# A two-layer block on one core: the first sequence's norm, first chunk and first four scans moved into the end of layer 0

## The chip, the cores and the metric

The kernel runs on one core of one Trainium2 chip. A core has five engines with an instruction queue each: TensorE (PE: matrix products, with PEld for its weight loads), VectorE (DVE), ScalarE (ACT), GpSimd (POOL) and SyncE (SP, which here only issues transfers). Each queue is worked off in its order; between queues there are semaphores. The metric is the device time of one execution in microseconds; lower is better.

## The reference, cut to what matters

Four sequences of 256 tokens with 512 features pass through two layers. `ln` is a layer norm without weights.

```python
# layer 0
xn = ln(x)
x = x + attention(xn) + (silu(xn @ Wg.T) * (xn @ Wu.T)) @ Wd.T      # 32 heads, 1792 hidden
# layer 1
xn = ln(x)
px, z = split(xn @ in_proj, 2)                       # 1024 channels each
xc = silu(conv4(px))                                 # causal, 4 taps along time
dt_r, B, C = rmsnorm of the three parts of xc @ x_proj.T      # 32, 16, 16
dt = softplus(dt_r @ dt_proj.T + dt_bias)
h[t] = exp(dt[t] * -exp(A_log)) * h[t-1] + dt[t] * B[t] * xc[t]   # 16 states per channel
y = (sum over states of h * C + D * xc) * silu(z)
x = x + y @ out_proj.T + experts(xn)                 # a dense product and 8 LoRA experts, top 2
```

The recurrence over time runs along the free dimension of one instruction, the scan.

## The kernel before, in words

The order of the work is written out by hand. In layer 0 generators hand out the products of the feed-forward part in small portions (`go(ff, n)`) between the steps of attention; `gate_up(th)` makes the hidden values of half `th` (two sequences), split into a high and a low part (hhi, hlo) that are multiplied in two passes. Its weights come in blocks of 128 hidden rows (tile wgu), loaded by POOL's queue through a ring of five tiles, four blocks ahead (`load_w`, L367). After both halves of `gate_up`, `down(th, i)` forms one block of 128 tokens: one product with the attention output (L404), 14 pairs of products (hhi and hlo, L409), and an addition to x on VectorE (L413). A portion is one pair, or the first product, or the addition: 16 portions a block, 64 for the four blocks of `down(1)`.

Those 64 portions are spread through the beginning of layer 1, which begins with the first two token blocks (the first sequence), whose x is already final. In order: statistics, root, scaling (`norm_stats`, `norm_scale`), transposing by TensorE and copying to xn1T (`norm_turn`, `norm_copy`); for four pairs of channel chunks p the products px (`px_mm`, L648), the convolution on ScalarE, VectorE and POOL (`conv_in` L656 to L664, `conv_taps` L672 and L678); silu; the decay rates aneg (L970) from the tile al, which 16 small transfers fill (L561); the product pp (`pp_mm` L692) and its norm; `step_in`, `step_exp`, `step_out`, `step_x` for dt and dt times xc (du).

A scan works on a step u: one chunk of 128 channels (c) and a quarter g of its 16 states. The 128 partitions of a step are 32 channels of four states, and four such groups lie along the free dimension, 4 x 256 values. So dt and du must be spread: `send` writes them to DRAM, and `spread` reads every row four times (L773, L779). Then `decays` makes the decay factors (ScalarE, L802), `scan_in` multiplies bx into PSUM (VectorE, L808), `scan` runs the recurrence (VectorE, L820) and multiplies by C (POOL, hc, L824), `states_sum` sums states by TensorE (ysum, L834 and L836) and `close_chunk` multiplies by the gate (L840). There are 32 steps for each sequence, 128 in all. The scheduled remainder of layer 1 (gates, products with z, the next sequence's norm and products) hangs on step numbers by `put(b, s, f, ...)`: f is issued at step s of sequence b.

What sets the order around the change: layer 0's tiles (pool l0: hidden values, wd) take up the memory into which the pool act goes, with two of three decay tiles, h, hc and the late weights rl, bw, lb, ow. So all 64 portions are issued before `l0.close()`, except for the last, which is an addition, and scan 0 follows. PSUM is a second tie: three buffers (psmm) hold all products of 512 values, whatever stage they belong to.

Of the kernel before, what the change touches and what calls it, by code (L numbers as in the profile page):

```python
# [28 lines left out]
NG = 4  # L29
# [12 lines left out]
def block_kernel(  # L42
# [52 lines left out]
    pssc = ps0.enter_context(tc.tile_pool(name="pssc", bufs=2, space=PSUM))  # L95
    psav = ps0.enter_context(tc.tile_pool(name="psav", bufs=1, space=PSUM))

    att = ExitStack()
# [133 lines left out]


    qs, kms = {}, {}

# [128 lines left out]
    def load_w(i):  # L364
        if i < 2 * NW:
            t = ffn.tile([P, HC, P], F32R, tag="wgu", name="wgu", bufs=5)
            nc.gpsimd.dma_start(t, wgu_d[i % NW // 2, :, i % 2])  # L367
            wgus[i] = t

    def gate_up(th):  # L370
# [4 lines left out]
        for m in range(MC):  # L375
            for k in range(2):
                i = th * NW + 2 * m + k
                load_w(i + 4)
                if th == 0 and k == 0 and m % 2 == 1:
# [76 lines left out]
    fold.close()  # L456
    for i in range(4):
        load_w(i)
# [62 lines left out]
    attention(2, ff, True, 10, 4)  # L521
    attention(3, ff, False, 10, 4)
    go(ff)
# [13 lines left out]
    PER = DC * NU  # L537
    xns, xcs, nrms, dts, szs, crows = {}, {}, {}, {}, {}, {}

# [5 lines left out]
    w_of = {}  # L545
    w_of["x", 0, 0] = weights(inx_d, 0)
    vec = w1.tile([P, DC, V_END], F32, name="vec")
    nc.sync.dma_start(vec, vec_d)
    w_of["x", 0, 1] = weights(inx_d, 2)
    xpw = w1.tile([P, DC, 64], F32, name="xpw")  # L550
    nc.sync.dma_start(xpw, xp_d)
    lnw = w1.tile([64, 1], F32, name="lnw")
    nc.sync.dma_start(lnw, lnw_d)
    dtw = w1.tile([RK, DIN], F32, name="dtw")
    nc.sync.dma_start(dtw, dtw_d)
    w_of["x", 0, 2] = weights(inx_d, 4)

    al = w1.tile([P, DC, NG, NST], F32, tag="u", name="al")
    for n in range(NG):
        for k in range(NG):  # L560
            nc.sync.dma_start(  # L561
                al[n * NB : (n + 1) * NB, :, k, :],
                vec_d[k * NB : (k + 1) * NB, :, V_AL : V_AL + NST],
            )
    aneg = w1.tile([P, DC, NG, NU], F32, name="aneg")
# [65 lines left out]
    def norm_turn(b, i):  # L631
# [3 lines left out]
        live["pt", b, i] = pt  # L635

    def norm_copy(b, i):
        if i == 0:
            xns[b] = odd(b).tile([P, HC, S], F32, tag="xn1T", name="xn1T")
        nc.scalar.copy(xns[b][:, :, i * P : (i + 1) * P], live["pt", b, i])  # L640
# [155 lines left out]


    def decays(u):
        b, c, g = u // PER, u % PER // NU, u % NU
        da = decay[u % len(decay)]  # L800
        for k in range(NG):
            nc.scalar.activation(da[:, k, 1:], live["dts", b, c][:, k, 1:], AF.Exp,  # L802
                                 scale=aneg[:, c, k, g : g + 1])
# [9 lines left out]
    def scan(u, parts=1):  # L813
        b, c, g = u // PER, u % PER // NU, u % NU
        da, bx = decay[u % len(decay)], live["bx"]
        h = act.tile([P, NG, S], F32, tag="h", name="h", bufs=2)
        hc = act.tile([P, NG, S], F32, tag="hc", name="hc", bufs=3)
        for k in range(parts):
            n = slice(k * NG // parts, (k + 1) * NG // parts)
            nc.vector.tensor_tensor_scan(  # L820
                h[:, n].rearrange("p n t -> p (n t)"), da[:, n].rearrange("p n t -> p (n t)"),
                bx[:, n].rearrange("p n t -> p (n t)"), 0.0, ALU.mult, ALU.add,
            )
            nc.gpsimd.tensor_tensor(  # L824
                hc[:, n], h[:, n],
                crows[b][:, g, :].unsqueeze(1).to_broadcast([P, NG // parts, S]), ALU.mult,
            )
        live["hc", u] = hc
# [17 lines left out]
    def router(b, i):  # L846
# [3 lines left out]
        for hc in range(HC):  # L850
            mm(pr, lhsT=xns[b + i // 2][:, hc, i % 2 * P : (i % 2 + 1) * P], rhs=rl[:, hc, :],
               start=(hc == 0), stop=(hc == HC - 1))
# [62 lines left out]
    def dense(b, i, k):  # L915
        if k == 0:
            live["po", b, i] = psmm.tile([P, D], F32, tag="mm", name="po1")
        for hc in (2 * k, 2 * k + 1):
            mm(live["po", b, i], lhsT=xns[b][:, hc, i * P : (i + 1) * P], rhs=bw[:, hc, :],
               start=(hc == 0), stop=False)  # L920

    def expert_out(b, i):
        mm(live["po", b, i], lhsT=ident, rhs=x[:, 2 * b + i, :], start=False, stop=False)
        mm(live["po", b, i], lhsT=live["mt"][:, i * P : (i + 1) * P], rhs=lb,
           start=False, stop=False)

    def out_mm(b, i, c):
        mm(live["po", b, i], lhsT=xcs[b][:, c, i * P : (i + 1) * P], rhs=ow[:, c, :],  # L928
           start=False, stop=(c == DC - 1))
# [13 lines left out]
    exp_set()  # L943
    norm_stats(0)
    ff = (0 for i in range(4) for _ in down(1, i))
    go(ff, 6)
    norm_scale(0)
    for i in range(2):
        norm_turn(0, i)
        norm_copy(0, i)  # L950
    go(ff, 3)
    for p in range(NP):
        for i in range(2):
            px_mm(0, p, i)
        conv_in(0, p)
        conv_taps(0, p)
        if p == 0:
            load_x(0, 3)
            for c in range(DC):
                nc.gpsimd.tensor_scalar(  # L960
                    dgs[:, c, :], ident, vec[:, c, V_D : V_D + 1], 1.0, ALU.mult, ALU.mult
                )
        elif p < 3:
            load_z(0, p - 1)
            go(ff, 4 - p)
    conv_silu(0)
    go(ff, 14)
    for n in range(NG):
        w = slice(n * NB, (n + 1) * NB)
        nc.scalar.activation(  # L970
            aneg[w], al[w].rearrange("p c k (g n) -> p c k g n", n=NG)[:, :, :, :, n], AF.Exp
        )
    nc.gpsimd.tensor_scalar(aneg, aneg, -1.0, 1.0, ALU.mult, ALU.mult)
    pp_mm(0, 0)
    pp_mm(0, 1)
    pp_square(0)
    pp_norm(0)
    go(ff, 6)
    for q in range(2):
        step_in(0, 0, q)  # L980
        step_exp(0, 0, slice(2 * q, 2 * q + 2))
        for k in range(3):
            step_out(0, 0, q, k)
        step_x(0, q)
        spread("dt", 0, q)
        spread("du", 0, q)
    b_rows(0, 0)
    c_rows(0, 0)
    go(ff, 4 * (MC + 2) - 35)
    scan_in(0)  # L990
    l0.close()
    act = ctx.enter_context(tc.tile_pool(name="act", bufs=1))
    decay_tile(act)
    decay_tile(act)
    bw = act.tile([P, HC, D], F32, name="bw")
    rl = act.tile([P, HC, NE + P], F32, name="rl")
    lb = act.tile([P, D], F32, name="lb")
    ow = act.tile([P, DC, D], F32, name="ow")
    nc.sync.dma_start(rl, rl_d)
    nc.sync.dma_start(bw, base_d)  # L1000
    nc.sync.dma_start(lb, lb_d)
    nc.sync.dma_start(ow, ow_d)

# [10 lines left out]
    for b in range(B):  # L1014
# [14 lines left out]
        else:  # L1029
            for p in range(2):  # L1030
                for i in range(2):
                    put(b, 2 * p + i, pz_mm, b, p, i)
        put(b, 0 if b else 3, gate_silu, b, 0, 1)

        put(b, 1, step_in, b, 1, 0)
        put(b, 2, step_in, b, 1, 1)
        put(b, 3 if b else 4, step_exp, b, 1)
        for q in range(2):
            for k in range(3):
                put(b, 5 + 3 * q + k, step_out, b, 1, q, k)  # L1040
        for p in (2, 3):
            put(b, 3 * p + 2, step_x, b, p)
        for c in range(2, DC):
            put(b, 4 * c - 6, spread, "dt", b, c)
            put(b, 4 * c - 4, spread, "du", b, c)
        put(b, 10, load_z, b, 2)
# [6 lines left out]
        if nxt < B:  # L1053
            put(b, 0, norm_stats, nxt)
            put(b, 2, norm_scale, nxt)
            put(b, 3, norm_turn, nxt, 0)
            put(b, 4, norm_copy, nxt, 0)
            put(b, 4, norm_turn, nxt, 1)
            put(b, 5, norm_copy, nxt, 1)
            for p in range(NP):  # L1060
                put(b, 2 * p, load_x, nxt, p)
                for i in range(2):
                    put(b, 6 + 2 * p + i, px_mm, nxt, p, i)
                put(b, 8 + 2 * p, conv_in, nxt, p)
                put(b, 9 + 2 * p, conv_taps, nxt, p)
            put(b, 16, conv_silu, nxt, (b, 2))
            put(b, 17, pp_mm, nxt, 0)
            put(b, 18, pp_mm, nxt, 1)
# [40 lines left out]
    late = []  # L1109
    decays(0)  # L1110
    decays(1)
    b_rows(0, 1)
    c_rows(0, 1)
    for u in range(total + 2):
        if u + 2 < total:
            decays(u + 2)
# [11 lines left out]
        if u < total:  # L1128
            scan(u, 1 if u < total - 1 else 4)
            if u == 0:  # L1130
                go(ff)
        for f, a in late_at.get(u, ()):
# [112 lines left out]
```

## Time and profile before

| | us |
|---|---|
| median of 3 runs | 901.28 (899.8 to 903.99) |
| the profiled execution, its own time | 900.89 |
| its span, first to last instruction | 899.1 |
| busy: PE, DVE, ACT, POOL | 751.5, 677.3, 523.3, 493.6 |
| last product of layer 0 ends | 379.42 |
| first scan starts | 380.02 |
| scan h (L820), x131 | 292.5, mean 2.235 |
| bx (L808), x128 | 157.6, mean 1.231 |
| hc (L824), x131 | 301.9, mean 2.307 |

Times in the profile count from the first instruction. A group's line gives source line, engine, operation, output and inputs by the program's names, the number of instructions, busy time, mean duration, and the idle time ahead of them with what ended it. A line of the timeline gives start and duration; neighbouring instructions of one kind are merged. One execution is profiled, so a difference is taken from its rows and carried over to the median of the runs.

### The profile page before, as it was taken

The numbers are of one execution on the slowest core, as the hardware profiler recorded it, in microseconds if no ns is written. First come the engines' busy times: TensorE is split into PE (matmuls) and PEld (weight loads), VectorE is DVE, ScalarE is ACT, GpSimd is POOL, SyncE is SP. The second block draws the span as 40 slices with busy tenths as digits, with TensorE's granted clock in tenths as the row PEclk, the third lists the DMA queues.
The fourth block names the chain that finished last, engine by engine and source line by source line (L and its number), as shares of the span: only waits on it lengthen the run. The fifth ranks groups of instructions, "written<-read, shape, count | busy, mean of one in ns | idle before, by whom it ended". The sixth has DMA issues, their size and how long they took to land.

```text
span 899.1 us, 10412 instructions
## 1 busy us (share of the span) xinstructions
PE 751.5 (84%) x3538; PEld 432.3 (48%) x3538; DVE 677.3 (75%) x660; ACT 523.3 (58%) x1004; POOL 493.6 (55%) x375
## 2 busy tenths in 40 slices
PE   5999979999989989967795798687898768975875
PEld 3665545666556666734452444343444434422321
DVE  5685553476662422298998999999999989999996
ACT  4234455313436445597677596777686785764661
POOL 4222222001223323459966879868789749697665
PEclk9899999999999999988886999887999888889997
DMA  7232232001123142593522543532546322437310
GB/s 222 60 93 71 82 107 71 12 1 36 47 59 82 47 106 69 143 280 95 162 80 62 156 132 111 139 95 88 159 128 161 83 82 74 117 95 167 86 28 24
DMA packets 68608, 87.98 MB, mean 98 GB/s; under 512 B 12190, under 2 KB 53418, under 8 KB 68171
## 3 DMA queue, kind: packets, MB, share of 16 engines
q1 hardware_dynamic: 59194, 68.44, 27.0%
q0 software_dynamic: 9072, 18.35, 7.3%
q8 instruction: 28, 0.46, 0.2%
q10 hardware_dynamic: 288, 0.52, 0.2%
q14 instruction: 26, 0.20, 0.1%
HBM read 67.63 MB, written 10.49 MB: 87 GB/s over the span
## 4 chain that ended last, share of the span: by engine, by line
PE 46%; DVE 30%; ACT 14%; issue 5%; POOL 4%; DMA 1%; SPq 0%; DVEq 0%; ACTq 0%; POOLq 0%
DVE h L820 18%; ACT decay L802 6%; PE po L409 6%; DVE bx L808 6%; PE pu L384 5%; PE pg L384 4%; PE sc L296 4%; PE av L338 3%; POOL hc L824 3%; PE scT L328 3%; PE pz L788 2%; PE pp L692 2%; PE px L648 2%; PE ysum L836 2%; PE po L928 2%
## 5 line engine op out<-in xcount | busy, mean ns | idle before, releaser
L824 POOL TENSOR_TENSOR hc<-h,cr 128x1024 f32<-128x1024 f32 (+1 forms) x131 | 301.9, 2307 | 110.2 <-DVE h L820 96.9
L820 DVE TENSOR_TENSOR_SCAN h<-decay,bx 128x1024 f32<-128x1024 f32 (+1 forms) x131 | 292.5, 2235 | 13.2 <-POOL hc L824 0.8
L802 ACT ACTIVATE decay<-dts,aneg 128x255 f32<-128x255 f32 x512 | 217.1, 498 | 123.9 <-DVE h L820 115.6
L808 DVE TENSOR_TENSOR bx<-brow,dus 128x1024 f32<-128x1024 f32 x128 | 157.6, 1231 | 9.0 <-DMA dus<-dud 5.2
L836 PE MATMUL ysum<-hc,stack 128*32 128x256 f32 x1024 | 89.9, 421 | 88.1 <-POOL hc L824 88.0
L396 POOL TENSOR_TENSOR hlo<-g,hhi 128x512 fp32r<-128x512 f32 x28 | 36.1, 1290 | 146.9 <-ACT hhi L395 146.9
L298 DVE TENSOR_REDUCE mpl<-sc 128x4 f32<-128x1024 f32 x64 | 77.2, 1222 | 23.9 <-PE sc L296 23.8
L836 PEld LDWEIGHTS ysum<-hc,stack 128*32 128x32 f32 x1024 | 21.5, 111 | 147.6 <-POOL hc L824 129.3
L367 POOL DMA_DIRECT2D wgu<-in_wgu x56 | 31.1, 557 | 92.4 <-PE pg L384 83.0
L330 ACT ACTIVATE pe<-scT 128x1024 f32<-128x1024 f32 x64 | 62.8, 1023 | 31.6 <-PE scT L328 31.4
L928 PE MATMUL po<-ow,xc 128*128 128x512 f32 x128 | 71.4, 667 | 2.7 <-DVE xc L840 2.7
L648 PE MATMUL px<-xn1T,w_in 128*128 128x256 f32 x256 | 67.5, 415 | 7.1 <-ACT xn1T L640 5.7
L788 PE MATMUL pz<-xn1T,w_in 128*128 128x256 f32 x256 | 66.7, 406 | 0.0
L648 PEld LDWEIGHTS px<-xn1T,w_in 128*128 128x128 f32 x256 | 52.4, 208 | 27.7 <-issue 10.4
L392 DVE SCALAR_TENSOR_TENSOR g<-g,pg 128x512 f32<-128x512 f32 x28 | 19.2, 684 | 55.0 <-ACT g L391 55.0
L788 PEld LDWEIGHTS pz<-xn1T,w_in 128*128 128x128 f32 x256 | 47.9, 197 | 18.8 <-issue 12.3
L395 ACT CAST hhi<-g 128x512 fp32r<-128x512 f32 x28 | 17.4, 620 | 61.0 <-DVE g L394 60.5
L384 PE MATMUL pg<-xhi,wgu 128*128 128x512 f32 x112 | 46.8, 418 | 5.5 <-issue 2.9
L409 PE MATMUL po<-wd,hhi 128*128 128x512 f32 x112 | 50.2, 448 | 0.0
L384 PE MATMUL pu<-xhi,wgu 128*128 128x512 f32 x112 | 47.6, 425 | 2.3 <-issue 1.5
L296 PE MATMUL sc<-km,qg 128*128 128x512 f32 x128 | 43.9, 424 | 3.3 <-ACT pe L330 2.8
L678 POOL TENSOR_TENSOR xc<-xc,tap 128x256 f32<-128x256 f32 x48 | 34.9, 727 | 21.0 <-ACT tap L664 18.5
(178 smaller groups left out, 1246.2 us busy)
## 6 DMA issues: line engine op xcount, KB each, us to landing
dts<-dtd SPq DMA_DIRECT2D x128, 128.0 KB, 2.8
dus<-dud SPq DMA_DIRECT2D x128, 128.0 KB, 3.0
wgu<-in_wgu POOLq DMA_DIRECT2D x56, 256.0 KB, 2.7
w_in<-in_inx SPq DMA_DIRECT2D x16, 512.0 KB, 4.7
w_in<-in_inz SPq DMA_DIRECT2D x16, 512.0 KB, 5.6
dtd<-dt SPq DMA_DIRECT2D x16, 256.0 KB, 2.3
dud<-du SPq DMA_DIRECT2D x16, 256.0 KB, 2.3
wd<-in_wd POOLq DMA_DIRECT2D x7, 512.0 KB, 3.6
```

Source lines behind the costliest of these rows:

```text
L296: mm(sc[:, hp, :], lhsT=qs[b][:, gq, hf, qb * P : (qb + 1) * P], rhs=kms[b][:, 2 * hp : 2 * hp + 2, :], start=True, stop=True)
L298: nc.vector.tensor_reduce(mpl2[b % 2][:, qb, :, 16 + 2 * gq + hf].rearrange("p (a i) -> p a i", a=2), sc.rearrange("p a (i k) -> p a i k", ...
L384: mm(ps, lhsT=wgus[i][:, hc, :], rhs=xs[j][:, hc, :], start=(hc == 0 and j == 0), stop=(hc == HC - 1 and j == 1))
L409: mm(po, lhsT=hids[th][j][:, m, i * P : (i + 1) * P], rhs=wd[:, m, :], start=False, stop=(m == MC - 1 and j == 1))
L648: mm(px[:, i, :], lhsT=w[:, i, hc, :], rhs=xns[b][:, hc, :], start=(hc == 0), stop=(hc == HC - 1))
L788: mm(pz[:, i, :], lhsT=w[:, i, hc, :], rhs=xns[b][:, hc, :], start=(hc == 0), stop=(hc == HC - 1))
L802: nc.scalar.activation(da[:, k, 1:], live["dts", b, c][:, k, 1:], AF.Exp, scale=aneg[:, c, k, g : g + 1])
L808: nc.vector.tensor_tensor(bx, brow[g // 2][:, g % 2, :].unsqueeze(1).to_broadcast([P, NG, S]), live["dus", b, c], ALU.mult)
L820: nc.vector.tensor_tensor_scan(h[:, n].rearrange("p n t -> p (n t)"), da[:, n].rearrange("p n t -> p (n t)"), bx[:, n].rearrange("p n t -> ...
L824: nc.gpsimd.tensor_tensor(hc[:, n], h[:, n], crows[b][:, g, :].unsqueeze(1).to_broadcast([P, NG // parts, S]), ALU.mult,)
L836: mm(ysum[k * NB : (k + 1) * NB, :], lhsT=stack, rhs=hc[:, k, :], start=False, stop=(g == NU - 1))
L928: mm(live["po", b, i], lhsT=xcs[b][:, c, i * P : (i + 1) * P], rhs=ow[:, c, :], start=False, stop=(c == DC - 1))
```

## The change

Three parts. The layer norm of the first sequence and its transposes move from the beginning of layer 1 into attention 3 of layer 0 (`pre_stats`, `pre_scale`, `pre_turn`, called between that attention's eight steps), with xn1T of the even sequences in a pool of its own; the weight ring of `gate_up` has four tiles and loads three blocks ahead. The first chunk's dt and du are no longer sent through DRAM: TensorE multiplies them with selection matrices (sel, in the tile of the conv taps), VectorE copies the results; the second chunk still goes through DRAM. The decay, h and hc of steps 0 to 3 lie in tiles borrowed from layer 1's weights and temporaries (`lend`), so that these scans need not wait for the pool act: 12 portions of `down` are issued with step 0, 12 with step 1, the remaining 8 with step 2, and `open_act` follows scan 2. To make room, much moves: the transfers into al, xpw, lnw and dtw are issued after px 0 and the fourth load of px weights; dgs ahead of the products; aneg ahead of the last pair's convolution, which is done without POOL; silu in two parts; the z weights and gates of the first sequence at steps 2 to 8; its second half of dt, and the next sequence's norm and products, one to three steps later.

```diff
+    def pre_stats(i):
+        ...
+        nc.vector.bn_stats(st, x[:, i, :])
+        nc.vector.bn_aggr(first_ln["mv"][:, i, :], st)
+    def pre_scale():
+        mv, rs = first_ln["mv"], first_ln["rs"]
+        nc.scalar.activation(rs[:, 0:2], mv[:, 0:2, 1], AF.Sqrt, bias=eps[:, 0:1])
+        nc.scalar.preload_act_table_set("exp_and_others")
+        nc.vector.reciprocal(rs[:, 0:2], rs[:, 0:2])
+        for i in range(2):
+            first_ln[i] = ap1.tile([P, D], F32, tag="ln_xn", name="xn", bufs=2)
+            nc.vector.tensor_scalar(
+                first_ln[i], x[:, i, :], mv[:, i, 0:1], rs[:, i : i + 1], ALU.subtract, ALU.mult
+            )
+    def pre_turn(i):
+        if i == 0:
+            xns[0] = pre.tile([P, HC, S], F32, tag="xn1T", name="xn1T")
+        pt = psmm.tile([P, HC, P], F32, tag="mm", name="pt")
+        for hc in range(HC):
+            nc.tensor.transpose(pt[:, hc, :], first_ln[i][:, hc * P : (hc + 1) * P], ident)
+        nc.vector.tensor_copy(xns[0][:, :, i * P : (i + 1) * P], pt)
...
-            t = ffn.tile([P, HC, P], F32R, tag="wgu", name="wgu", bufs=5)
+            t = ffn.tile([P, HC, P], F32R, tag="wgu", name="wgu", bufs=4)
...
-                load_w(i + 4)
+                load_w(i + 3)
...
-    attention(3, ff, False, 10, 4)
+    attention(3, ff, False, 10, 4, [(pre_stats, 0), (pre_stats, 1), (pre_scale,), (pre_turn, 0),
+                                    (pre_turn, 1)])
...
-    w_of["x", 0, 0] = weights(inx_d, 0)
+    for i in range(2):
+        nc.sync.dma_start(t[:, i], inx_d[:, i])
...
-    al = w1.tile([P, DC, NG, NST], F32, tag="u", name="al")
+    al = w1.tile([P, NG, DC, NST], F32, tag="u", name="al")
+    def load_rest():
+        for n in range(NG):
+            for k in range(NG):
+                nc.sync.dma_start(
+                    al[n * NB : (n + 1) * NB, k],
+                    vec_d[k * NB : (k + 1) * NB, :, V_AL : V_AL + NST],
+                )
+        nc.sync.dma_start(xpw, xp_d)
+        ...
...
+    lent = {
+        "d": ("d", "w_in", "d", "w_in"), "h": ("w_in", "u", "w_in", "u"),
+        "hc": ("w_in", "lw", "e", "lw"),
+    }
...
-    norm_stats(0)
     ff = (0 for i in range(4) for _ in down(1, i))
-    go(ff, 6)
-    norm_scale(0)
-    for i in range(2):
-        norm_turn(0, i)
-        norm_copy(0, i)
-    go(ff, 3)
+    go(ff, 9)
+    for c in range(DC):
+        nc.gpsimd.tensor_scalar(
+            dgs[:, c, :], ident, vec[:, c, V_D : V_D + 1], 1.0, ALU.mult, ALU.mult
+        )
     for p in range(NP):
         for i in range(2):
             px_mm(0, p, i)
         if p == 0:
             load_x(0, 3)
+            load_rest()
+        if p < 3:
+            conv_in(0, p)
+            conv_taps(0, p)
+            go(ff, 1)
...
...
+    px = live["px", 0, 3]
+    nc.scalar.copy(pads[1][:, :, KC - 1 :], px)
+    for i in range(2):
+        v = vec[:, 6 + i, :]
+        nc.scalar.activation(px[:, i, :], px[:, i, :], AF.Identity, bias=v[:, V_CB : V_CB + 1],
+                             scale=v[:, V_CW + KC - 1 : V_CW + KC])
+    for i in range(2):
+        for k in range(KC - 1):
+            nc.vector.scalar_tensor_tensor(
+                px[:, i, :] if k < KC - 2 else xcs[0][:, 6 + i, :], pads[1][:, i, k : k + S],
+                vec[:, 6 + i, V_CW + k : V_CW + k + 1], px[:, i, :], ALU.mult, ALU.add,
+            )
+    nc.scalar.activation(xcs[0][:, 0:6, :], xcs[0][:, 0:6, :], AF.Silu)
+    nc.scalar.activation(xcs[0][:, 6:8, :], xcs[0][:, 6:8, :], AF.Silu)
...
+    go(ff, 8)
     pp_mm(0, 0)
     pp_mm(0, 1)
     pp_square(0)
     pp_norm(0)
+    go(ff, 4)
+    step_in(0, 0, 0)
+    for j in range(2):
+        step_exp(0, 0, slice(j, j + 1))
     b_rows(0, 0)
     c_rows(0, 0)
+    for j, eng in ((0, nc.vector), (1, nc.gpsimd)):
+        eng.tensor_tensor(e[:, j, :], u[:, j, :], e[:, j, :], ALU.subtract)
+        eng.tensor_tensor(e[:, j, :], e[:, j, :], lw[:, j, :], ALU.add)
+        eng.tensor_tensor(dt[:, j, :], dt[:, j, :], e[:, j, :], ALU.add)
+        eng.tensor_tensor(du[:, j, :], dt[:, j, :], xcs[0][:, j, :], ALU.mult)
+    go(ff, 8)
+    pdts = psx.tile([P, NG, S], F32, tag="bx", name="pdts")
+    for k in range(NG):
+        mm(pdts[:, k, :], lhsT=sel[:, k * P : (k + 1) * P], rhs=dt[:, 0, :], start=True, stop=True)
+    nc.vector.tensor_copy(live["dts", 0, 0], pdts)
+    for i in range(2):
+        pdu = psmm.tile([P, 2, S], F32, tag="mm", name="pdus")
+        for k in range(2):
+            mm(pdu[:, k, :], lhsT=sel[:, (2 * i + k) * P : (2 * i + k + 1) * P], rhs=du[:, 0, :],
+               start=True, stop=True)
+        nc.vector.tensor_copy(live["dus", 0, 0][:, 2 * i : 2 * i + 2, :], pdu)
...
+    decays(0)
     scan_in(0)
+    spread("dt", 0, 1)
+    spread("du", 0, 1)
+    b_rows(0, 1)
+    c_rows(0, 1)
+    step_in(0, 0, 1)
+    step_exp(0, 0, slice(2, 4))
+    decays(1)
...
-    decays(0)
-    decays(1)
-    b_rows(0, 1)
-    c_rows(0, 1)
     for u in range(total + 2):
-        if u + 2 < total:
+        if u < 3:
+            go(ff, 12 if u < 2 else 100)
+        if 3 <= u < total - 2:
             decays(u + 2)
...
             scan(u, 1 if u < total - 1 else 4)
-            if u == 0:
-                go(ff)
+            if u == 2:
+                open_act()
+            if u < 3:
+                decays(u + 2)
```

Of the schedule, the steps of `put` move as told above.

## The prediction, made before the changed kernel was run

> **What bounds the kernel now.** I read the page first, then busy time by stretch, the chain that ended last between 312 and 383 us, each engine in order of time there, and the waits of VectorE. Below: busy time by stretch (columns: length, then busy time and instructions of PE, its weight loads, DVE, ACT, POOL, then TensorE clock, DMA share, GB/s).
>
> ```profile
> 315.00:379.40 64.40, 59.40 (x236) 44.03 (x234) 13.82 (x28) 34.29 (x63) 23.62 (x34) 0.95 0.38 101
> 379.40:420.00 40.60, 30.96 (x169) 19.10 (x169) 36.31 (x28) 34.95 (x73) 28.43 (x17) 0.83 0.74 218
> 420.00:892.00 472.00, 368.59 (x1849) 183.33 (x1848) 449.24 (x359) 326.32 (x688) 366.34 (x209) 0.89 0.38 106
> ```
>
> From 315 to 379.4 TensorE is busy for 59.4 of 64.4 us and VectorE for 13.8; afterwards VectorE is busy for 449 of 472 us. So the time is (end of layer 0's last product, "E", 379.42) plus a VectorE queue. The chain shows where TensorE's 64.47 us from 314.95 to E go (start, length, work):
>
> ```profile
> 319.14 3.24 issue
> 322.38 1.79 PE pt L634 x8
> 324.17 2.27 PE po L409 x6
> ...
> 340.40 3.69 PE px L648 x16
> ...
> 351.31 3.61 PE pp L692 x16
> ...
> 361.70 1.06 PE brow L713 x4
> 362.76 0.86 PE pcr L718 x4
> 363.62 7.69 PE po L409 x26
> ```
>
> The reader sees 3.24 us of waiting for the norm, its transposes (1.79), and products slowed behind them: 2.27 for six matmuls, where six take 1.39 at 333.35. VectorE in order of time at E:
>
> ```profile
> 379.91 0.18 DVE L614 BATCH_NORM_AGGREGATE mv<-st 128x2 f32<-128x6 f32 x1
> 380.02 2.29 DVE L820 TENSOR_TENSOR_SCAN h<-decay,bx 128x1024 f32<-128x1024 f32 x1
> 382.22 0.66 DVE L413 TENSOR_TENSOR x<-x,po 128x512 f32<-128x512 f32 x1
> 382.80 1.22 DVE L808 TENSOR_TENSOR bx<-brow,dus 128x1024 f32<-128x1024 f32 x1
> ```
>
> Scan 0 starts only at 380.02, scan 2 ends at 390.18. Last, the SP queue, and VectorE's waits after E:
>
> ```profile
> 321.43 14.33 SPq L561 DMA_DIRECT2D al<-in_vec  x16
> ```
> ```profile
> DVE px L672 <- ACT xc L659: 2.3, 1, 2.3
> DVE h L820 <- POOL hc L824: 0.8, 1, 0.8
> ```
>
> Sixteen small transfers occupy the SP queue for 14.33 us, 2.5 of them one wait for a weight transfer: 0.74 each.
>
> **What the Trainium skill says.** "TensorE: Matmul & The Clock Gate", Part 1: the array runs at half clock after an idle window of about 3.4 us and gets it back after a busy one. The trace agrees: after the idle 3.24 us the granted clock is 0.51 from 322.5 to 326. It is also 0.51 from 363.5 to 367, right behind the small-row products pdt, brow and pcr (3.84 us); each stretch costs about 1.7 us. "ScalarE: Activation LUTs", What ACT_TABLE_LOAD costs: 1283 ns for any set; here the loads take 1.28. "DMA: Bandwidth & Descriptors", Why small descriptors are slow: a fixed overhead per packet; 16 KB of al took 2.4 us to land where 256 KB of wgu took 2.7.
>
> **The change part by part.** Times from one profiled execution: 900.89 us, span 899.1, so 1.8 lie around the span; the median of runs, 901.28, is 0.4 above it. I carry differences over to the median.
>
> *Before the down products.* Eight 128x128 transposes enter attention 3 on TensorE, which is dense there: 8 x 0.166 (four took 0.66 at 392.58) = +1.3. VectorE's pieces (two stats pairs 1.7, two scalings and two copies about 0.7 each) fit its gaps of over 2 us; ScalarE's two table loads and root (2.9) delay the next exponentials by 1.3 us, and their score buffers have about 2 us of slack: 0, up to 1.6 without that cover. The weight ring shrinks from 5 to 4 and loads go 3 blocks ahead. In attention a block lasts about 4 us, so three cover the 2.7 us to land. The last load (pu of m=13) is now issued behind the hlo of m=11, which ended at 311.36: 311.36 + 2.6 = 314.0 against 313.13 for its block: +0.9 (0 to 1.5). Sum +2.2.
>
> *Down products until E.* Gone: idle 3.24, transposes 1.79, slow pairs 2.27 - 1.39 = 0.88, px's wait for a tap 1.29: -7.2. Added on TensorE: spreading by sel, 16 instructions of 0.217 (px: 3.47 per 16) = 3.5; rows for steps 2 and 3 (brow 1.06, pcr 0.86), which came after E, 1.9; the first ysum 1.2 (0.63 + 0.57). The first w_in half can only be issued when the last hlo ends, 2.9 after the start of po, and lands at 5.6 to 6.0; TensorE arrives at 5.6 (4.2 for the first five pairs, three more at 0.46): +0.45. Now the new wait. On SP the al loads moved behind load_x(0,3), which waits for px 0 to be read (5.6 + 0.45 + 3.5 = 9.5 after the start): 9.5 + 0.5 + 15 x 0.74 + 2.4 = 23.5. On ScalarE the aneg exponentials stand in front of the scaling of px 3, which TensorE finished at 21.2. What is queued behind them: aneg's last 0.43, pad 0.6, two scalings 1.1 (to 25.7); then VectorE's six taps of 0.5 (to 28.7), on which pp waits for its PSUM buffer. TensorE, with six pairs and one m_att behind px 3, is free at 25.7: +3.05. The destination of al is contiguous now; if that halves the issue time, the wait is about 1.1, so I take the pace seen. Behind al on SP stand xpw, lnw and dtw, which land near 25: in time for pp at 28.7. On POOL dgs (8 x 0.35) now stands ahead of the first taps: done at 10.3, the taps come at 11.6. Sum 10.1 - 7.2 = +2.9; E is 2.2 + 2.9 = 5.1 later, at about 384.5.
>
> Dropped for the first chunk: stores, reads back (du's spread landed at 377) and their waits; they delayed scan 0, not E. Chunk 1 keeps its four transfers, ahead of its use by over 20 us. POOL does that chunk's four operations (0.73 each) and the first step_out before hc of scan 0, done about 54.5 where TensorE asks for it at 61: hidden; an hc later than that would stop the down products themselves.
>
> *After E.* Scan 0's inputs are ready some 47 us after the start of po, so scans 0 and 1 run before E. Scan 2 does not: in VectorE's order the last x add, waiting for E, stands before bx 2, and so do the next norm's stats. From E to the end of scan 2 it took 10.76; it becomes 0.7 + 1.6 + 1.3 + 2.35 = 5.95: -4.8. The late weights (3.5 MB) go out at E as before, now beside z's first load and chunk 2; z lands some 5 us after E, gate and close are needed at 14.7: hidden. Without that, VectorE stands at the first close.
>
> *Steps 5 to 17.* step_in, step_exp, step_out sit three steps later, the gate takes two silu switches of table instead of one (+2.6 on ScalarE). Following ScalarE's queue (decays 1.65 each, step_in 1.5 twice, step_exp 4.4, switch and gate 3.1 twice, xnt 1.5), conv_in of px(1,0) ends about 36.6 after E, VectorE reaches it at 32.2: 4.4 idle, where 3.16 stood: +1.2 (-3 to +4).
>
> Sum: 2.2 + 2.9 - 4.8 + 1.2 = **+1.5 us**: 902.4 for a profiled execution, 902.8 for the median.
>
> **The rivals.**
> *A, slower.* The wait before pp grows and cools the array. At 14.33/16 = 0.9 per al load it is 5.4, beyond 3.4 us, so a half-clock stretch of 1.7 follows, and two more can follow the two groups pdt, brow, pcr. That is +2.4 + 3 x 1.7 = 7.5 on E: 910. It decides from 3 us beyond my sum (905.8). For it: both half-clock stretches above. Against it: the groups are now 2.9 us, under the 3.84 that triggered, and al's slow stretch held a foreign wait.
> *B, faster.* al issues at about 0.45, the wait vanishes (-3.05), and conv_in, a step later, no longer holds VectorE (-4.4): 895.3. For it: the idle before was the ScalarE chain, and taps now come one step later. Against it: ScalarE's two queues worked out above.
> *C, POOL becomes the bound.* Steps 8 to 14 now hold hc 7 x 2.35, six step_out of 1.27, two du of 1.28, three tap groups of 2.33: 33.6 us against VectorE's 31.2. With two h buffers about 2.6 of lag is free; if the hc start late too, +3 to +5: 907. Against it: step_exp comes later, so no hc stands behind e, as one did before (0.8).
> *D, the early scans gain nothing* since TensorE's end sets all: then -4.8 is lost, 907.6. Against it: from 420 VectorE is 95% busy, so scans moved out of it count. I put D's chance with C's.
>
> **How the numbers follow.** 0.5% (4.5 us, 896.8 to 905.8) is about what a measurement of this kernel can tell from no change. My forecast with its bounds (al's pace -2, clock +-1.7, ring -0.9 to +0.6, idle +-2; about 898.5 to 905.5) has 0.56, A 0.20, B 0.13, C with D 0.11. Same: 0.55 and a little of B and C, 0.59. Faster: most of B and a little of the forecast, 0.13. Slower: A and most of C and D, 0.28. The range leaves out B's half below 897 and the tail of A above 909.5.
>
> **What would show it.** Right: no wait before the first px; scan 0 near 363 and scan 1 before E, scan 2 right behind the last x add and stats; E near 384.5; a gap of about 3 us before pp ending on ScalarE and VectorE, with al landing late on SP; about 4 us idle of VectorE before px(1,0)'s taps. Wrong: E at 381 or earlier (B), half clock around pp and the second pcr with E beyond 388 (A), scans after step 8 waiting for hc (C), or scan 2 before E.

## The result and the profile after

| | before | after |
|---|---|---|
| median of 10 runs, us | 899.59 (898.03 to 903.99) | 906.05 (902.86 to 908.5) |
| ratio | 1 | 1.0071, 95% interval 1.0052 to 1.0089 |
| profiled execution, its span | 900.89, 899.1 | 906.83, 905.0 |
| first down product (T0) | 314.95 | 316.37 |
| last product of layer 0 (E) | 379.42 | 381.76 |
| scan 0, scan 2 start | 380.02, 387.89 | 363.23, 385.35 |
| scan 10, scan 22, scan 127 start | 421.98, 470.64, 888.38 | 426.01, 477.03, 893.85 |

The changed kernel is 0.7% slower, by 6.5 us in the medians (5.9 in the profiled executions) where 1.5 was forecast. The scans that were to gain start earlier: scan 2, in spite of a later E, by 2.5 us. All of that and more is lost afterwards: scan 8 is still 1.2 ahead, scan 17 is 5.3 behind.

Busy time by stretch, after (columns as in the prediction; the stretches are T0 to E, E to 420, the rest):

```profile
316.40:381.80 65.40, 62.44 (x261) 45.55 (x259) 23.37 (x35) 36.26 (x72) 23.86 (x34) 1.00 0.26 66
381.80:420.00 38.20, 28.36 (x146) 18.39 (x147) 30.98 (x24) 28.00 (x53) 20.25 (x13) 0.82 0.86 246
```

Up to E things are better than forecast: the granted clock is 1.00 throughout (0.95 before). From E to 420 VectorE is busy for 31.0 of 38.2 us, where it was 36.3 of 40.6. The chain of work around pp, after:

```profile
322.51 3.71 PE px L689 x16
...
336.86 2.15 DMA al<-in_vec
...
342.60 1.49 ACT xc L1040
344.09 0.43 issue
344.52 3.65 PE pp L733 x16
```

and the SP queue, after:

```profile
326.60 10.87 SPq L596 DMA_DIRECT2D al<-in_vec  x16
```

The al transfers take 10.9 us (0.68 each, 0.74 forecast) and land at 339.0; pp starts late as forecast, but by 1.8 us instead of 3.05. VectorE's waits from E to scan 22, after (line, what it waited for, total, times, longest):

```profile
DVE px L713 <- ACT xc L700: 5.9, 2, 4.7
DVE x L446 <- PE po L442: 5.0, 1, 5.0
DVE xc L901 <- PE ysum L897: 4.7, 2, 2.8
DVE nrm L747 <- ACT rs L645: 1.0, 1, 1.0
```

The second line is the wait for E itself. The other three, 11.6 us, stand against 3.1 before; these 8.5 us are nearly all of the 8.9 that the way from scan 2 to scan 22 has grown by. The first line is called the tap wait below: VectorE waits for ScalarE's part of the convolution of the next sequence. The two waits of the third line are new in kind: the gate that closes a chunk waits for its sum over states, which is TensorE's. So TensorE in order of time behind E, after (last column: idle ahead of it and what ended that):

```profile
388.52 5.85 PE L829 MATMUL pz<-xn1T,w_in 128*128 128x256 f32 x16 [6.76 <-DMA w_in<-in_inz]
394.29 1.07 PE L897 MATMUL ysum<-hc,stack 128*32 128x256 f32 x16
...
401.57 4.46 PE L829 MATMUL pz<-xn1T,w_in 128*128 128x256 f32 x16
405.95 1.13 PE L772 MATMUL pdt<-nrm,dtw 32*128 32x256 f32 x4
```

and ScalarE there:

```profile
407.12 0.47 ACT L777 ACTIVATE u<-pdt,vec 128x256 f32<-128x256 f32 x1 [4.23 <-PE pdt L772]
...
416.66 1.28 ACT L835 ACT_TABLE_LOAD   x1
...
421.47 0.56 ACT L697 COPY pad<-px 128x512 f32<-128x512 f32 x1
```

TensorE waits 6.8 us for the first z weights and does both pz slowly (5.85 and 4.46, with a granted clock of 0.50 from 388.5 to 391; 16 such products take 3.62 in a run below). ysum 1 and 2, the second half's pdt and the transposes stand behind pz in its queue. The second pdt comes only at 405.95, and from it ScalarE has 14 us of work (step_in, step_exp, three decays, the second gate with its two table loads) before the pad of the next sequence's first convolution, for whose taps VectorE waits.

### The profile page after: what moved, and what is told of

Read it like the earlier page. It is cut to its first block, busy times and chain, and to the rows that moved or that the text cites. A ratio compares the mean times of both kernels' runs of the same rounds, so it can differ in the third digit from the quotient of the medians.

```text
span 905.0 us, 10447 instructions
## 1 busy us (share of the span) xinstructions
PE 755.9 (84%) x3554; PEld 433.7 (48%) x3554; DVE 686.4 (76%) x675; ACT 525.5 (58%) x1005; POOL 489.4 (54%) x374
## 4 chain that ended last, share of the span: by engine, by line
PE 40%; DVE 32%; ACT 13%; POOL 6%; issue 5%; DMA 2%; SPq 1%; DVEq 0%; ACTq 0%; POOLq 0%
DVE h L881 19%; DVE bx L866 6%; ACT decay L860 5%; PE po L442 5%; PE pu L417 4%; PE pg L417 4%; PE sc L329 4%; POOL hc L885 3%; PE av L371 3%; PE scT L361 3%; PE pz L829 2%; PE pp L733 2%; PE ysum L897 2%; PE po L989 1%; ACT pe L363 1%
## 5 line engine op out<-in xcount | busy, mean ns | idle before, releaser
L881 DVE TENSOR_TENSOR_SCAN h<-decay,bx 128x1024 f32<-128x1024 f32 (+1 forms) x129 | 288.0, 2234 | 11.7
L860 ACT ACTIVATE decay<-dts,aneg 128x255 f32<-128x255 f32 x504 | 213.9, 499 | 117.8 <-DVE h L881 114.8
L897 PE MATMUL ysum<-hc,stack 128*32 128x256 f32 x1024 | 92.2, 431 | 89.5 <-POOL hc L885 89.2
L829 PE MATMUL pz<-xn1T,w_in 128*128 128x256 f32 x256 | 72.3, 433 | 6.8 <-DMA w_in<-in_inz 6.8
L689 PE MATMUL px<-xn1T,w_in 128*128 128x256 f32 x256 | 64.6, 400 | 2.3 <-ACT xn1T L681 1.6
L829 PEld LDWEIGHTS pz<-xn1T,w_in 128*128 128x128 f32 x256 | 52.1, 213 | 28.4 <-issue 12.2
L417 PE MATMUL pg<-xlo,wgu 128*128 128x512 f32 x112 | 44.8, 400 | 0.0
```

The lines of the kernel that those rows point to most:

```text
L417: mm(ps, lhsT=wgus[i][:, hc, :], rhs=xs[j][:, hc, :], start=(hc == 0 and j == 0), stop=(hc == HC - 1 and j == 1))
L689: mm(px[:, i, :], lhsT=w[:, i, hc, :], rhs=xns[b][:, hc, :], start=(hc == 0), stop=(hc == HC - 1))
L829: mm(pz[:, i, :], lhsT=w[:, i, hc, :], rhs=xns[b][:, hc, :], start=(hc == 0), stop=(hc == HC - 1))
L881: nc.vector.tensor_tensor_scan(h[:, n].rearrange("p n t -> p (n t)"), da[:, n].rearrange("p n t -> p (n t)"), bx[:, n].rearrange("p n t -> ...
L897: mm(ysum[k * NB : (k + 1) * NB, :], lhsT=stack, rhs=hc[:, k, :], start=False, stop=(g == NU - 1))
```

## The experiments

Theory T: the late load of z stops TensorE, and the rest follows from that. Rival R1: the steps that were moved behind one another (second half of dt, second gate) fill ScalarE's and POOL's queues, whenever z comes. In that first form it did not speak of TensorE, whose order counted as part of T; from the run with pz at 9 on, R1 takes in TensorE's queue (second pz ahead of the second half of dt). Rival R2: z is slow because it shares the DMA engines with the late weights.

One measure for all, from the start times in each trace: T0 to E, and E to the start of scan 22. These two come from one profiled execution of each kernel, the medians and ratios from all runs; in brackets is the median of the kernel before in the same series. From T0 to E the changed kernel and its variants do nearly the same, and gave 65.0 to 67.9; the second column was 95.3 and 93.3 in two kernels with the same code after E. So a single trace doesn't tell differences below some 2 us there. Four of the profiled executions were slow ones of their kernel: z first, gate at 10, the shift alone and the norm part alone lie 2.6 to 3.1 above the median.

| kernel | T0 to E | E to scan 22 | median, us (before) | ratio to before, 95% |
|---|---|---|---|---|
| before | 64.5 | 91.2 | - | 1 |
| after | 65.4 | 95.3 | 906.05 (899.59) | 1.0071 (1.0052 to 1.0089) |
| z first | 67.9 | 93.4 | 908.15 (900.02) | 1.0081 (1.0059 to 1.0103) |
| late weights at step 9 | 65.8 | 93.0 | 905.67 (900.02) | 1.0063 (1.0050 to 1.0076) |
| own hc 3 | 67.7 | 96.5 | 910.08 (900.02) | 1.0115 (1.0100 to 1.0129) |
| al on two queues | 65.3 | 93.3 | 907.30 (900.02) | 1.0087 (1.0072 to 1.0102) |
| gate at 10 | 67.6 | 92.1 | 903.88 (899.32) | 1.0057 (1.0040 to 1.0074) |
| gate at 10, pz at 9 | 66.0 | 88.5 | 902.19 (899.32) | 1.0021 (1.0006 to 1.0035) |
| these with z, late weights, al | 65.3 | 85.9 | 898.26 (899.32) | 0.9988 (0.9975 to 1.0001) |
| before, schedule shift alone | 65.8 | 100.0 | 906.36 (899.32) | 1.0072 (1.0044 to 1.0101) |
| before, norm part alone | 57.4 | 92.4 | 896.68 (900.95) | 0.9955 (0.9940 to 0.9970) |
| all mended, scan 2 before E | 65.2 | 83.9 | 897.01 (900.95) | 0.9962 (0.9944 to 0.9980) |
| and the next norm before E | 65.0 | 82.3 | 894.25 (898.92) | 0.9938 (0.9917 to 0.9960) |
| norm part, pp earlier | 59.8 | 92.4 | 898.41 (898.92) | 0.9991 (0.9976 to 1.0006) |

**z first.**

```diff
+            put(b, 2, load_z, b, 0)
             for k in range(3):
                 put(b, k, step_out, b, 0, 1, k)
             put(b, 2, step_x, b, 1)
-            put(b, 2, load_z, b, 0)
```

> The changed kernel with one line moved: at step 2 the first load of z's weights is issued ahead of the two stores (dtd, dud) that wait for POOL. Its tile is free at 371.4 us, so it should land near 375, before the last product of layer 0 (E, 381.8). Theory T (the late z weights stop TensorE, and ysum 1 and 2, hc 3 and both half steps of step_in stand behind pz in its queue): pz follows E at once instead of 6.8 us later, hc of scan 3 starts near 391.3 instead of 395.05, VectorE's waits for ysum at the first two closes (1.98 and 2.77) go, the wait for px's first tap (4.7) shrinks; about 899 to 901 us against 906. Rival R1 (the steps that were moved three later and the second silu switch fill ScalarE and POOL, whenever z comes): only the first close's 2 us go, the tap wait stays near 4.5; 904.

z was there in time and pz followed E at once, in 3.62 us. The time did not fall. TensorE in order of time and VectorE's waits after E, with z first:

```profile
386.78 3.62 PE L829 MATMUL pz<-xn1T,w_in 128*128 128x256 f32 x16
390.33 0.64 PE L897 MATMUL ysum<-hc,stack 128*32 128x256 f32 x8
395.32 1.08 PE L897 MATMUL ysum<-hc,stack 128*32 128x256 f32 x8 [4.35 <-POOL decay L626]
```
```profile
DVE px L713 <- ACT xc L700: 6.3, 1, 6.3
...
DVE xc L901 <- PE ysum L897: 1.9, 1, 1.9
DVE nrm L747 <- ACT rs L645: 1.8, 1, 1.8
```

One wait of TensorE is gone (6.8), another took its place (4.35: ysum 2 needs hc 2, whose scan runs only after E; hc 2 ended at 395.26, and the name in the view is that of the small memset behind it on POOL). The first close no longer waits, the second does, and the tap wait is 6.3 instead of 4.7. So less came of it than even R1's 904. T by itself falls: the late z is real, but not alone what sets the time.

**Late weights at step 9.**

```diff
-            nc.sync.dma_start(late_w[n], d)
+            put(0, 9, nc.sync.dma_start, late_w[n], d)
```

> The changed kernel with the 3.5 MB of late weights (rl, bw, lb, ow) issued at step 9 instead of right after scan 2; order of z's load untouched (issued 382.4). Theory R2 (z's load is slow because it shares the DMA engines with the late weights: it took 6.1 us from issue to landing): it lands in about 3, at 385.4, TensorE's wait falls from 6.8 to about 3.7, and about 3 us of the time go: 903. If the landing stays at 6, the load is held by something else: 906. The late weights may be missed later (out to +2 around step 16).

The DMA issues between 380 and 396 us there (size of one, median us from issue to landing):

```profile
w_in<-in_inz SPq DMA_DIRECT2D x1, 512.0 KB, 6.0
dts<-dtd SPq DMA_DIRECT2D x4, 128.0 KB, 6.1
```

z's first load takes 6.0, as with the late weights beside it (issued at 382.43, landed at 388.4), and TensorE still waits 6.8. R2 falls for this load. The second one landed 5.1 us after its issue instead of 7.0, but nothing waited for it in either kernel. What else z's load shares the engines with are the spread reads of dts and two stores; that these slow it was not tried.

**Own hc 3.** `lent["hc"]` loses its fourth entry, and hc of scan 3 comes from the pool act.

> The changed kernel with the hc of scan 3 in the pool act instead of the tile lw borrowed from hc 1. Theory T says that hc 3 waits (391.3 to 395.05) because ysum 1, which frees lw, stands behind pz: hc 3 starts at 391.3, but its ysum is still behind pz and two other ysums (395.9), so the first close waits 0.5 to 1 us instead of 1.98, and later waits hardly move: -1 us, 905. If the borrowed tile itself is the cause of the close's wait: -2 or more at the first close and the second close's wait (2.77) falls too, 902.

hc 3 then follows scan 3 at once and the first close waits 1.0, as expected; the second waits 4.9, behind a second pz that waited 3.6 us for z's second load, and the tap wait is 6.3. Relieving one wait moved the loss to the next, and the time, 910, is above both expectations. Part of it is the slow pp described at the end. z's second load was issued 13.2 us after E (12.6 in the changed kernel) and took 8.2 us to land (7.0 there); why is open.

**Al on two queues.** Eight of the 16 transfers go to POOL's queue ahead of dgs.

> The changed kernel with half of al's 16 loads on POOL's queue ahead of dgs instead of on SP. al lands near 334 instead of 339, the last pair's pad follows px 3 at 338 instead of 339.6, and TensorE's wait before pp falls from 1.8 to about 0.3: E 1.5 earlier, 904.5 us. If E doesn't pass on (rival: what counts after E is TensorE's order and ScalarE's queue), E is 1.5 earlier and the time the same.

TensorE's wait before pp fell from 1.8 to 1.25, not to 0.3, since silu and its table load still stand there. The time did not fall, as the expectation's rival had it.

**Gate at 10; gate at 10 and pz at 9.** The first lines below belong to the second run alone.

```diff
-            for p, u in ((0, 2), (1, 6)):
+            for p, u in ((0, 2), (1, 9)):
...
-            put(b, 8, gate_silu, b, 1)
+            put(b, 10, gate_silu, b, 1)
```

> The changed kernel with the second gate's silu (two table switches, 3.16 us on ScalarE) at step 10 instead of 8, behind the first convolution of the next sequence. Rival R1 (ScalarE's queue, with the second half of step_exp and the second gate in front of that convolution, holds VectorE): the tap wait falls by about 3 (4.7 to 6.3 seen so far, to 1.7 to 3), 903 us. Theory T (the late z weights and TensorE's order): the tap wait only moves to the next wait for px or ysum, 905 to 906.

> As before it, and the second product pz, which stands in TensorE's queue in front of the second half's pdt, also goes behind the first px (step 9 instead of 6). R1 with TensorE's order: pdt 402.6 instead of 406, step_exp and the convolution's pad 3 to 4 us earlier again, so no tap wait and no wait at the second close (2.77): 7 us less between scan 2 and scan 22, 899 us. If only the switch counts, as the run with the gate alone.

VectorE's waits with the gate alone, and with the gate and pz:

```profile
DVE px L713 <- ACT xc L700: 3.6, 2, 3.0
DVE xc L901 <- PE ysum L897: 2.9, 2, 2.4
```
```profile
DVE xc L901 <- PE ysum L897: 2.4, 1, 2.4
...
DVE px L713 <- ACT xc L700: 0.6, 1, 0.6
```

The gate alone is 3.2 us shorter from E to scan 22 than the changed kernel but only 1.2 than the run with al on two queues, and the intervals of the ratios overlap: it is too small to be told by itself. The two together are 6.7 (or 4.8) shorter, and the ratio falls clear of the changed kernel's, though z is as late as ever (TensorE waits 6.4). With pz behind the first px, the second pdt reaches ScalarE at 404.9 instead of 407.1, 21.4 instead of 25.4 us after E. This is R1 in its wider form, with both queues: pz ahead of pdt on TensorE, the gate ahead of the convolution on ScalarE. The expected 899 was missed, 902.19: 1.8 of the 6.7 were lost ahead of E in the profiled execution, 0.7 behind scan 22. The wait of 2.4 that is left is at the first close, where the late z still tells.

**All of these together.** Gate, pz, z first, late weights at 9, al on two queues.

> The gate and pz later, together with z's first load first, the late weights at step 9 and half of al on POOL's queue. R1: VectorE has no wait for taps or closes left beyond 2 us between scan 2 and scan 22; E as in the changed kernel or 1 earlier: 896 to 898 us, faster than before. If 902 or more, something else than these waits sets the time there.

From E to scan 22 it is 9.4 us shorter than in the changed kernel, and the time equals the kernel before; the wait at the first close is gone with z early, so T has a share of some 2 us. The expected 896 to 898 was a little missed (898.26).

**The shift alone, in the kernel before.** The diff is that of the schedule in the change (step_in at 5 and 6, step_exp at 7, gates at 4 and 8, pz at 2 and 6, the next sequence one later); z is loaded early, as before.

> The kernel before with one part of the change alone: the later steps of the schedule (second half of dt three steps later, gates at 4 and 8, pz at 2 and 6, the next sequence's norm, products and convolution one later); its own early z weights, spread through DRAM and late first scan kept. R1: VectorE's tap wait grows from 2.3 to 5 or more although z is early, +3 to +5 us, 904. Theory T: the shift costs nothing without the late z load, 900 to 901.

```profile
DVE px L672 <- ACT xc L659: 5.9, 2, 4.7
DVE xc L840 <- PE ysum L836: 3.3, 1, 3.3
DVE nrm L706 <- ACT rs L606: 1.0, 1, 1.0
```

VectorE's waits after E are nearly those of the changed kernel, without borrowed tiles or a late z; only the first close doesn't wait. On TensorE the second half's pdt stands behind pz as there:

```profile
404.07 4.64 PE L788 MATMUL pz<-xn1T,w_in 128*128 128x256 f32 x16
408.64 1.13 PE L731 MATMUL pdt<-nrm,dtw 32*128 32x256 f32 x4
```

From E to scan 22 the shift costs 8.8 us in this execution: 7.1 more of these waits, and 1.6 of the next norm's statistics on VectorE, which it moves out of the wait for E to behind scan 1. The time is 0.7% longer, 7.0 us in the medians, more than the 3 to 5 expected. R1 is shown from both sides: moving the gate and pz away gives back most of what the changed kernel lost, and the schedule put into the kernel before costs as much as the whole change.

**The norm part alone, in the kernel before**, with the ring of four and al behind the last px weights.

> The kernel before with one part of the change alone: the first sequence's norm and transposes in attention 3, with the ring of four weight tiles, and the al transfers behind the last px weights; dt and du still through DRAM, all scans after the last product, the schedule as before. By the prediction's prices: 3.24 idle, 1.79 transposes and 0.88 of slow products go (5.9), 2.2 come in front of the down products: E 3.7 us earlier (375.7 against 379.4) and the whole time with it, 896 us. Rival D (E does not set the time, what follows waits for something else): E 3.7 earlier, the time within 1 us of before, 899.

T0 to E is 7.05 shorter, the whole faster by 0.45%, about as expected. In the profiled execution E itself is only 2.55 earlier, for T0 came 4.5 later, 3.5 of them already at the end of attention 3. VectorE at scan 0 in that run:

```profile
376.35 1.23 DVE L834 TENSOR_TENSOR bx<-brow,dus 128x1024 f32<-128x1024 f32 x1 [6.87 <-DMA dus<-dud]
...
379.11 2.29 DVE L846 TENSOR_TENSOR_SCAN h<-decay,bx 128x1024 f32<-128x1024 f32 x1
```

E is at 376.87, and scan 0 starts 2.2 behind it (0.6 before): du's way through DRAM now ends as late as E, and the statistics come after it.

**The rest of the change, mended further.** In the kernel with all of these together, scan 2 is put ahead of the last addition to x, with the next norm's statistics and scaling behind that addition; in a further kernel the statistics go behind scan 1 and the scaling behind scan 2. The further one's lines:

```diff
...
-            go(ff, 12 if u < 2 else 100)
+            go(ff, 12 if u < 2 else 7)
...
             if u == 2:
+                norm_scale(1)
+                go(ff)
                 open_act()
+            if u == 1:
+                norm_stats(1)
```

> The run with gate, pz, z, late weights and al together, and scan 2 (with its bx) ahead of the last x addition, in VectorE's 5 us of waiting for E; the next norm's statistics and scaling right behind that addition. Scan 3 starts 3.6 us earlier relative to E. If VectorE's queue alone sets the end: 3.6 us faster, 894.7. By ScalarE's queue, whose work between E and the next convolution (some 26 us without idle) does not shrink: a tap wait of about 2.5 comes back, 896. Either way at or below 897 and faster than before.

> As the run with scan 2 ahead of the last x addition, with the next norm's statistics behind scan 1 and its scaling behind scan 2, so that 1.7 us of VectorE and 2.0 of ScalarE lie before E (sequence 1's x is final since the first half of the down products). From E to scan 22 took 83.9 there. If ScalarE's queue after E holds VectorE: its 2 us of tap waits go, and VectorE has 1.7 less to do: 80.5, the time 893.5 us. If the tap wait stays, only VectorE's 1.7: 895.3.

VectorE in order of time in the second of them (E is 381.79):

```profile
376.69 0.67 DVE L652 BATCH_NORM_STATS2 st<-x 128x6 f32<-128x512 f32 x1
...
378.29 1.21 DVE L866 TENSOR_TENSOR bx<-brow,dus 128x1024 f32<-128x1024 f32 x1
379.63 2.29 DVE L881 TENSOR_TENSOR_SCAN h<-decay,bx 128x1024 f32<-128x1024 f32 x1
381.83 0.14 DVE L661 SCALAR_TENSOR_TENSOR sh<-mv,rsn 128x2 f32<-128x2 f32 x1
381.89 0.67 DVE L446 TENSOR_TENSOR x<-x,po 128x512 f32<-128x512 f32 x1
```

The wait of 5.0 for E is filled. From E to scan 22 took 1.6 less than in the first of the two, as much as the statistics take on VectorE, though two traces can differ by that; the tap wait stayed near 2. The first came to 897.01, 0.4% faster than before, the second to 894.25, 0.6% faster than before and 1.3% faster than the change as it was made.

**Norm part, pp four portions earlier, statistics ahead of bx 0.**

> As the run with the norm part alone, with pp four portions earlier and the next norm's statistics ahead of bx 0. There scan 0 started 2.2 us after E, because bx 0 waited for du's way through DRAM and the statistics (1.7) came behind it. Scan 0 then starts 0.1 to 0.5 after E: 1.8 us faster, 895 us. If the decays or rows hold scan 0 instead: no change, 896.7. Set against the kernel with all parts mended, it tells what spreading by TensorE and the four early scans are worth.

Scan 0 came 0.2 after E as expected, but T0 to E grew by 2.3: pp now waits 1.3 for silu, and a down product 0.8 for VectorE. Missed: 898.41, no faster than before. What spreading by TensorE and the early scans are worth above the norm part can't be told with these runs: 0.9938 (to 0.9960) against 0.9955 (from 0.9940). The norm part's 0.45% gained and the shift's 0.7% lost make up 0.3% of loss, not the 0.7% of the whole change; what the rest of the change costs as it was made was not taken apart further.

## Why the prediction was right or wrong

The forecast, within 0.5% at 902.8, was wrong in kind: the change is slower by over 0.5%, a case given 0.28. That the time, 906.05, still lies below 909.5 is luck. Behind scan 2 it went some 7 us worse than forecast; of this, 2.8 were offset by errors of the opposite sign ahead of E, and 1.7 by the kernel before, whose median came down from 901.28 (three runs) to 899.59 (ten).

*Before the down products, +2.2.* T0 moved by 1.4. The late last weight block is there (0.93 of waiting; 0.9 forecast). The transposes can't be read from one trace: the point just before it, the end of attention 3's last products, lay between 303.6 and 306.9 us in runs of the same code.

*T0 to E, +2.9; measured +0.9.* The norm part alone shows -7.05 where -7.2 was to go, but as a balance: some 1.5 more went with a slow stretch (next paragraph), and a new wait of 1.57 stood before the first px, for its weights. Of the additions, sel (1.73 twice for 3.5), rows (1.92 for 1.9), ysum (1.0 for 1.2) and the first weights (0.62 for 0.45) are right. Mis-sized was the wait before pp, 1.8 for 3.05, since al went out faster. Left out was a gain: the slow stretch behind pdt, brow and pcr, eight products in 3.5 us where they take 2.0, did not come again. Of some 1 us the other way, 0.35 is the transposes, which had held TensorE for 1.44 us (322.38 to 323.82) and not 1.79; the rest is spread over small rows.

The prediction laid that slow stretch to the length of its group, 3.84 us then and 2.9 after the change. That does not hold. In the norm part alone the same group stands there with the same length, 358.68 to 362.52:

```profile
358.68 1.99 PE L757 MATMUL pdt<-nrm,dtw 32*128 32x256 f32 x8
360.60 1.13 PE L739 MATMUL brow<-nrm,bcsel 64*128 64x256 f32 x4
361.57 1.02 PE L744 MATMUL pcr<-nrm,bcsel 64*128 64x256 f32 x4
```

The stretches behind it, in the kernel before and in the norm part alone (the third number from the end is the clock):

```profile
363.50:367.00 3.50, 3.50 (x9) 2.77 (x9) 0.00 (x0) 3.44 (x8) 2.46 (x2) 0.51 0.00 0
```
```profile
362.00:370.00 8.00, 8.00 (x34) 5.86 (x32) 0.69 (x1) 6.39 (x12) 6.33 (x5) 1.00 0.13 45
```

With pp earlier it is 1.00 too behind this group, with the shift alone, whose code is that of the kernel before up to E, it fell to 0.50 again. What sets the stretch off stays open.

*From E to scan 2, -4.8; measured -4.9.* Scans 0 and 1 ran before E, scan 2 right behind the addition and the statistics.

*Steps 5 to 17, +1.2 (-3 to +4); measured +7.8 from scan 2 to scan 17, +8.9 to scan 22.* This is the step that failed. It followed ScalarE's queue alone, and on that got the tap wait nearly right, 4.4 for 4.7. But the agreement is chance: ScalarE's convolution ended 41.4 us after E, not 36.6, and VectorE reached its taps at 36.8, not 32.2. Both were held some 4.7 us longer by TensorE, whose queue after E was not followed: pdt of the second half stands behind pz there, as the run with pz at 9 shows, and the ysums of the chunks stand behind both, which gave two waits at the closes, 4.7 in all; 1.2 and 1.0 came later. "Hidden" was written of z because gate and close came much later; that other work is queued behind pz was not asked. An early z alone would not have saved it, since the shift costs as much with z early.

*The rivals.* A, slower, named the wrong place: E came at 381.8, not beyond 388. Its mechanism did occur in three variants, below. B falls (al at 0.68, the tap wait stayed). C falls: no scan waited for hc. D said that the early scans gain nothing because TensorE's end sets all. The reason is not that, since scan 2 was 2.5 ahead; but for the change as a whole their gain was given back by what was moved to make room for them.

## What to carry to other kernels

When work is moved later to make room, follow the in-order queue of every engine past the move, TensorE's too, and ask of each product what stands behind it: here the second half of dt stood behind a pz that nobody needed yet, and moving that product and one gate behind the next convolution took some 5 to 7 us off the way from E to scan 22. Test a bundle by its parts in both directions: the norm part alone gained 0.45%, the moved schedule alone lost 0.7%, and the bundle showed one number. And work that depends on nothing late (the next norm's statistics) belongs in the wait for the end of a stage, not behind it: moved behind it, it was 1.6 of the 8.8 us of the shift.

## What the hardware showed unexpectedly

The wait in front of pp sometimes cost a second time. TensorE in order of time in the run with the gate at 10, and in that with pz at 9 too:

```profile
345.39 5.32 PE L733 MATMUL pp<-xc,xpw 128*64 128x256 f32 x16 [2.16 <-ACT xc L1040]
```
```profile
346.29 3.64 PE L733 MATMUL pp<-xc,xpw 128*64 128x256 f32 x16 [2.54 <-ACT xc L1040]
```

After waits of 2.16, 2.49 and 2.81 us in this place the same 16 products took 5.2 to 5.3 us, after 1.25, 1.81, 2.35 and 2.54 they took 3.64. The granted clock was 0.51 from 345.4 to 348.8 in the first of the two runs shown, 1.00 through pp in the second. T0 to E was 67.6 to 67.9 in the three, 65.0 to 66.0 in the changed kernel's other variants. The Trainium skill, "TensorE: Matmul & The Clock Gate", Part 1, tells of half clock after an idle window of about 3.4 us; here it set in after 2.2 to 2.8 us of waiting, and not every time. Of the five waits between 2.16 and 2.81 us, three cost 1.6 to 1.7 us more. And behind pdt, brow and pcr it set in with no wait of TensorE beyond 0.5 us in the 20 us before.
